# Edge messages of a graph layer: pairs of edges on a partition, gathers without a wait for TensorE, a deeper order of weighing and summing

## The chip, the cores and the metric

The kernel runs on one core of a Trainium2 chip. The time is the device time of one execution in microseconds. Shown are 4624.53, 4624.89 and 4639.22 us, with a median of 4624.89 us, and one execution taken by the profiler, 4628.1 us.

Engines are called as in the profile: PE (TensorE, matmuls; PEld its weight loads), DVE (VectorE), ACT (ScalarE), POOL (GpSimd) and SP (SyncE). SBUF is the working memory, PSUM the memory into which TensorE writes. A semaphore is a counter by which one engine tells another that something is done.

## The reference

12500 nodes with 128 features, and 412500 edges: 200000 random ones in both directions, and one edge from each node to itself. The edges are sorted by their target `dst`, so a target has 33 edges in a row on average.

```python
theta = x[dst] - x[src]
w = sigmoid(relu(theta @ W1 + b1) @ W2 + b2)          # one number for each edge
agg = segment_sum(w * theta, dst, num_segments=n_nodes)
indeg = segment_sum(ones, dst, num_segments=n_nodes)
x = layernorm(x + agg + indeg * (x @ W4 + b4))
```

All is in 32-bit floats. An edge from a node to itself has theta = 0 and adds nothing to `agg`, and 1 to `indeg`.

## The kernel before

**Tables.** `theta @ W1` is `y[dst] - y[src]` with `y = x @ W1`, so `y` is computed once for all nodes. `z` in DRAM holds y and x of a node side by side (1 KB), `y3d` holds y split in three bf16 parts, from which a bf16 matmul makes the full value again.

**Parts and blocks.** The sorted edges are cut into parts, and two parts are a block (`SUB`). A block has a window of 96 consecutive targets (`WB`). The first 20 parts (`PLAIN`) have 1024 edges each. Each later part takes CE = 1182 consecutive edges: 1024 of them are laid out as 8 tiles (`K`) of 128 edges, an edge to a partition, and up to 128 others are "hot": edges whose source is one of the first 2304 nodes, whose rows lie in SBUF (`tabs`), so that they need no gather. Edges from a node to itself are dropped (except for the first 20 parts). There are 352 parts, 351 whole ones and a tail.

**Planning.** Which edge of a part goes where is computed on the chip, by `place` (L451), in sets of 128 parts, a part to a partition. It finds the hot edges (`max` and `match_replace` on 1182 columns, L511 and L513), counts how far each remaining edge has to move, moves them by powers of two (L572 to L576), and hands out `src_i` (the sources, for the gathers), `rel` (the target within the window) and the rows `off_d` (the target within the part), which are read back from DRAM, broadcast to all partitions, as `to_all` (L688). It is a generator, and the main loop takes a step of it now and then.

**One part,** in the main loop over s (L1069 on):

- `gather(s + 4)` (L335 to L353): eight indirect DMAs issued by POOL, each with 128 rows of z into one tile of a buffer. There are nine such buffers, `zbuf`, used in turn.
- `one_hot(s + 2)` (L772, L773): ACT makes from `to_all` a matrix that picks each edge's target, |offset - place| and then 1 - that, cut at zero, for 8 tiles and one of hot edges, 1152 columns.
- `spread_y(s + 1)` (L781): eight matmuls that bring y of the target to each edge, into `ph` (PSUM, two buffers).
- `one_hot_w(s)` (L791): DVE compares the target in the window with 0 to 95, 768 columns.
- `weights(s)`: DVE subtracts the gathered y (L824), masks and multiplies with W2 (L825), sums over the features (L828); ACT makes the sigmoid, once for the multiplication (`gate`, L829), once as a column of `wx` (L830).
- `weigh(s)` (L839): DVE multiplies the gathered x with the weight into `wx` (two buffers). It is the last to read the part's zbuf.
- `add_up(s - 1)` (L940): eight matmuls sum the weighted rows by target into `pa`, one more adds the hot edges, and in a block's second part one carries on the sums of targets that the last block shared (`sh`). A 32-bit matmul is two instructions in the profile. `total` copies `pa` to SBUF (L951).
- `hot_weights(s + 1)` (L915 to L920), `hot_rows(s + 2)` (L904, L905), and every four parts `hot_fetch` (L884, L891, L895), which picks 512 hot rows by 27 matmuls.
- once in a block `own_u` (L707 to L714) for the targets' own term, and `normalize` (L963 to L990), which finishes the block two before.

**Order.** SP's queue is in the order of the program; a scheduler of the language arranges the other engines' instructions ahead of time by its own estimate, and every engine runs its own in that fixed order. Loads of a block are issued on SP two blocks ahead (L670 to L698). POOL's queue holds nothing but gathers. They are paced by hand: each gather of part s is made to wait for an instruction of TensorE that belongs to the work of part s - 6:

```python
if s - LAG >= NH and (s - LAG, k) in steps_of:
    waits.append((steps_of[s - LAG, k], mybir.DependencyClass.Sync))
```

`step(...)` writes these instructions down in own_u, spread_y, hot_rows and add_up.

Of the kernel before, what the change touches and what calls it, by code (L numbers as in the profile page):

```python
# [19 lines left out]
P = 128  # L20
D = 128
K = 8
BE = K * P
# [7 lines left out]
NZ = 9  # L31
AHEAD = 4
LB = 6
LAG = 6
# [8 lines left out]
RW = BE + HK  # L43
# [5 lines left out]
CE = 1182  # L49
# [7 lines left out]
def gnn_resnorm(  # L57
# [45 lines left out]
    KT = -(-TAIL // P)  # L103
    assert NS == NF + 1 and NS % SUB == 0 and TAIL <= BE and SUB == 2 and N < BIG

# [36 lines left out]
    def load(i):  # L142

        s0, n, full = sets[i]
        es = ep.tile([P, CE], I32, name="es")
        ed = ep.tile([P, CE + 1], I32, name="ed")
        e0 = E1 + (s0 - PLAIN) * CE
        if full < n:
            nc.vector.memset(es[:n, :], 0)
            nc.vector.memset(ed[:n, :], N)  # L150
# [68 lines left out]
    oh_buf = [const.tile([P, K + 1, P], BF16, name=f"oh{i}") for i in range(2)]  # L219
# [78 lines left out]
    wx_buf = [const.tile([P, K, AW], F32, name=f"wx{i}") for i in range(2)]  # L298
# [3 lines left out]
    wxh_buf = [const.tile([P, AW], F32, name=f"wxh{i}") for i in range(3)]  # L302
# [15 lines left out]
    def tiles(s):  # L318
        return K if s < NF else KT
# [9 lines left out]
    steps_of = {}  # L329
    table_steps = []  # L330

    def step(s, i, ins):

        steps_of[s // SUB * SUB + i // K, i % K] = ins

    def gather(s):

        (src_i, _, _), i = set_of(s)
        for k in range(tiles(s)):
# [7 lines left out]
            if s - LAG >= NH and (s - LAG, k) in steps_of:  # L347
                waits.append((steps_of[s - LAG, k], mybir.DependencyClass.Sync))
# [92 lines left out]
    def place(i, ps, es, ed, bb):  # L441
# [9 lines left out]
        c = ep.tile([P, 6], F32, name="col")[:n]  # L451
# [9 lines left out]
        v.tensor_scalar(b[:full, 1:2], c[:full, 3:4], -1.0, float(CE - BE - HR * HS),  # L461
                        op0=OP.mult, op1=OP.add)
# [5 lines left out]
        t = ep.tile([P, CE], F32, name="et")[:n]  # L468
        nc.scalar.activation(t, ed[:, :CE], AF.Identity, scale=float(BIG), bias=c[:, 0:1])
        C = CE // 3  # L470
        for j in range(3):
            at = slice(j * C, (j + 1) * C)
            step = ps.tile([P, G, P], F32, name=bank).rearrange("p g d -> p (g d)")[:n, :C]
            v.tensor_sub(step, ed[:, j * C + 1:(j + 1) * C + 1], ed[:, at])
            q = ep.tile([P, P * G], F32, name="eq")[:n, :C]
            v.tensor_sub(q, es[:, at], ed[:, at])
            v.tensor_mul(q, q, step)
            v.scalar_tensor_tensor(t[:, at], step, 0.0, t[:, at], op0=OP.is_equal, op1=OP.mult)
# [11 lines left out]
        key = ep.tile([P, CE + 1], F32, name="ed")[:n, :CE]  # L490
# [3 lines left out]
        for r in range(HR):  # L494
            apart = aparts[r][:n]
            whole = CE // PM * PM
# [3 lines left out]
                apart.rearrange("p (o m) -> p o m", o=1).to_broadcast([n, CE // PM, PM]), op=OP.add)  # L500
            if whole < CE:
                v.tensor_tensor(key[:, whole:], t[:, whole:], apart[:, :CE - whole], op=OP.add)
# [32 lines left out]
        nc.sync.dma_start(rows_d[:n, BE:], hd[:, 1, :])  # L535
        hots[s0] = hot_s, hrel, n

        w = ep.tile([P, CE], I32, name="ew")[:n]
        C = CE // 6
        for j in range(6):  # L540
            at = slice(j * C, (j + 1) * C)
            pw = ps.tile([P, G, P], F32, name=bank).rearrange("p g d -> p (g d)")[:n]
            count = pw[:, :C]
            q = ep.tile([P, P * G], F32, name="eq")[:n]
            keep, out_ = q[:, :C], q[:, C:2 * C]
# [4 lines left out]
            v.tensor_tensor_scan(count, out_, most[:n].to_broadcast([n, C]),  # L550
                                 c[:, 4:5] if j else 0.0, op0=OP.add, op1=OP.min)
            v.tensor_copy(c[:, 4:5], count[:, C - 1:])
            move = out_.bitcast(I32)
            far_on = pw[:, C:2 * C]
# [6 lines left out]
        v.tensor_sub(b[:full, 10:11], c[:full, 4:5], c[:full, 3:4])  # L561
        v.tensor_scalar(b[:full, 10:11], b[:full, 10:11], -float(HR * HS), None, op0=OP.add)
        v.tensor_scalar(b[:full, 11:12], b[:full, 10:11], -1.0, None, op0=OP.mult)
        assert SW + HR * HS < LAST + P
        for r, m in enumerate([1 << r for r in range(7)] + [LAST]):
            u = ep.tile([P, CE], I32, name="ew" if r % 2 else "et")[:n]
            C = bits.shape[1] - m
            for c0 in range(0, CE, C):
                c2 = min(c0 + C + m, CE)
# [9 lines left out]
                if c2 == CE:  # L579
                    break  # L580
            w = u
        to = ep.tile([P, CE + 1], I32, name="ed")[:n, :BE]
        v.tensor_scalar(to, w[:, :BE], BIG.bit_length() - 1, 2 * NOT - 1,
                        op0=OP.logical_shift_right, op1=OP.bitwise_and)
        off = ep.tile([P, P * G], F32, name="eq").bitcast(BF16)
        nc.scalar.activation(off[:n], to, AF.Identity, bias=c[:, 1:2])
        nc.sync.dma_start(rows_d[:n, :BE], off[:n])
        yield
        t = ep.tile([P, CE], F32, name="et")[:n]
        nc.scalar.activation(t[:, :BE], to, AF.Identity, bias=c[:, 2:3])  # L590
        src_i = pp.tile([P, K, P], I32, name="src_i")
        rel = pp.tile([P, K, P], BF16, name="rel")
        f = ep.tile([P, CE], F32, name="es")[:n]
# [3 lines left out]
        for e, to in ((f, src_i), (t, rel)):  # L597
            for k0 in range(0, K, G):
                pt = ps.tile([P, G, P], F32, name=bank)
                for j in range(G):  # L600
                    nc.tensor.transpose(pt[:, j, :n], e[:, (k0 + j) * P:(k0 + j + 1) * P],
                                        ident[:n, :n])
                nc.scalar.activation(to[:, k0:k0 + G, :n], pt[:, :, :n], AF.Copy)
# [3 lines left out]
    with tc.manual_schedule(engines={SP}), tc.tile_pool(name="work", bufs=2) as wp, tc.tile_pool(  # L607
# [94 lines left out]
        def own_u(b):  # L702
# [3 lines left out]
            step(b * SUB - 2, 2,  # L706
# [593 lines left out]
```

## Time and profile before

| | |
|---|---|
| median of 3 runs | 4624.89 us (4624.53 to 4639.22) |
| profiled execution | 4628.1 us, span 4626.2 us |
| PE busy, PEld busy | 2636.8 us (57%), 1988.8 us (43%) |
| DVE busy | 3121.2 us (67%) |
| ACT busy | 1603.8 us (35%) |
| POOL busy | 2681.1 us (58%), 2815 gathers |
| TensorE clock granted, mean | 0.729 |
| moved by DMA | 539.42 MB, 117 GB/s |

The clock of TensorE is at all times either whole or half, and 0.729 is the mean. A group's row gives line, engine, operation, tile written and tiles read, sizes, count, then busy time and the mean of one in ns, then the idle time of the engine before these instructions, with what ended most of it. "issue" is time in which the engine waited for nothing that the profile shows. "remote" stands where a semaphore rose and the profile found no instruction that ended at that moment. A line of the waits has who waited, for whom, the total in us, how many times, and the longest.

### The profile page before, as it was taken

How to read it: one execution, taken by the hardware profiler on the slowest of the kernel's cores; microseconds unless marked ns; L12 is line 12 of the kernel's file. 1: busy time of each engine (PE TensorE's matmuls, PEld its weight loads, DVE VectorE, ACT ScalarE, POOL GpSimd, SP SyncE). 2: the span in 40 equal slices, each digit the busy share in tenths (PEclk: the TensorE clock that was granted, in tenths of full speed). 3: DMA queues.
4: the chain of work that ended last, by engine and by line, in shares of the span. 5: the costliest groups of instructions: out<-in, count | busy, mean ns of one | idle time of the engine just before them, and what ended most of it. 6: DMA issues, size and time to landing. Idle time of an engine off the chain costs nothing. (4 is left out here: it accounts for less than half of the span.)

```text
span 4626.2 us, 47225 instructions
## 1 busy us (share of the span) xinstructions
PE 2636.8 (57%) x14207; PEld 1988.8 (43%) x14207; DVE 3121.2 (67%) x5030; ACT 1603.8 (35%) x3344; POOL 2681.1 (58%) x2824
## 2 busy tenths in 40 slices
PE   4355556665655555655565655556555556555555
PEld 4344344444444444444444444444444444444444
DVE  5676667777776666666777776777666566566666
ACT  4233333333333333333333333333333333333333
POOL 4415656666565566665556656656656565655663
PEclk6676777767777777777777777776777777777777
DMA  6303433443443344434333433434433443333432
GB/s 247 111 28 108 126 115 114 122 121 112 118 122 110 109 125 122 120 114 122 112 118 116 121 109 115 123 111 123 121 112 112 121 120 117 116 116 114 120 113 67
DMA packets 269164, 539.42 MB, mean 117 GB/s; under 512 B 101349, under 2 KB 152737, under 8 KB 267365
## 3 DMA queue, kind: packets, MB, share of 16 engines
q0 software_dynamic: 134096, 364.95, 27.2%
q1 hardware_dynamic: 132834, 164.97, 11.2%
q10 hardware_dynamic: 1970, 6.40, 0.5%
q8 instruction: 115, 1.88, 0.2%
q14 instruction: 149, 1.21, 0.1%
HBM read 504.19 MB, written 31.90 MB: 116 GB/s over the span
## 5 line engine op out<-in xcount | busy, mean ns | idle before, releaser
L340 POOL DMA_INDIRECT zbuf<-z,src_i x2655 | 2524.2, 951 | 1645.1 <-issue 695.5
L940 PE MATMUL pa<-wx,ow 128*96 128x130 f32 x5630 | 1125.8, 374 | 847.3 <-ACT a L951 339.9
L940 PEld LDWEIGHTS pa<-wx,ow 128*96 128x96 f32 x5630 | 1006.2, 238 | 953.9 <-ACT a L951 366.8
L839 DVE TENSOR_TENSOR wx<-zbuf,fix 128x1024 f32<-128x1024 f32 x352 | 427.3, 1214 | 601.0 <-ACT fix L829 449.2
L772 ACT ACTIVATE oh<-to_all,away 123x1152 bf16<-123x1152 bf16 x332 | 415.7, 1252 | 689.8 <-remote 350.2
L891 PE MATMUL pd<-of,tabs 128*128 128x512 bf16 (+1 forms) x2322 | 543.1, 385 | 91.2 <-issue 90.7
L791 DVE TENSOR_TENSOR ow<-fix,rel 128x768 f32<-128x768 f32 x352 | 333.5, 947 | 300.3 <-remote 296.7
L884 DVE TENSOR_TENSOR of<-hot_src,fix 128x1536 bf16<-128x1536 f16 (+1 forms) x258 | 422.2, 1690 | 10.8 <-remote 8.6
L828 DVE TENSOR_REDUCE lg<-ph 128x8 f32<-128x1024 f32 x352 | 427.0, 1213 | 0.0
L824 DVE TENSOR_TENSOR ph<-ph,zbuf 128x1024 f32<-128x1024 f32 x344 | 420.2, 1222 | 8.8 <-issue 3.2
L904 PE MATMUL pw<-wni,xT 128*128 128x256 f32 x664 | 301.7, 548 | 210.1 <-ACT wxh L918 106.2
L825 DVE SCALAR_TENSOR_TENSOR ph<-ph,w_r 128x1024 f32<-128x1024 f32 x344 | 420.7, 1223 | 0.0
L891 PEld LDWEIGHTS <-tabs 128*128 128x128 bf16 x2322 | 233.1, 101 | 363.3 <-issue 150.5
L773 ACT ACTIVATE oh<-oh 123x1152 bf16<-123x1152 bf16 x332 | 384.1, 1157 | 6.4
L781 PE MATMUL ph<-y,oh 128*128 128x128 bf16 x2751 | 261.0, 244 | 180.5 <-DVE lg L828 121.3
L781 PEld LDWEIGHTS <-oh 128*128 128x128 bf16 x2751 | 215.7, 111 | 246.5 <-issue 211.5
L915 DVE SCALAR_TENSOR_TENSOR hh<-pw,w_r 128x128 f32<-128x128 f32 x332 | 92.6, 279 | 285.5 <-PE pw L905 181.2
L940 PE MATMUL pa<-a,sh 96*96 96x130 f32 x350 | 106.2, 398 | 287.7 <-issue 85.4
L963 ACT ACTIVATE pw<-xw,sw 96x128 f32<-96x128 f32 x176 | 64.6, 367 | 545.2 <-issue 241.4
L904 PEld LDWEIGHTS pw<-wni,xT 128*128 128x128 f32 x664 | 142.7, 266 | 246.4 <-ACT wxh L918 135.9
L895 ACT ACTIVATE xT<-pd 128x512 f32<-128x512 f32 (+1 forms) x86 | 50.1, 582 | 481.6 <-PE pd L891 388.4
L951 ACT ACTIVATE a<-pa 96x130 f32<-96x130 f32 x176 | 47.8, 272 | 459.4 <-remote 398.5
(257 smaller groups left out, 2925.5 us busy)
## 6 DMA issues: line engine op xcount, KB each, us to landing
to_all<-off_d SPq DMA_DIRECT2D x166, 576.0 KB
zbuf<-z,src_i POOLq DMA_INDIRECT x2655
z<-zbuf SPq DMA_DIRECT2D x12, 1024.0 KB
y<-y3d SPq DMA_DIRECT2D x342, 30.8 KB
y3d<-tabs SPq DMA_DIRECT2D x12, 768.0 KB
xw<-in_x_dram SPq DMA_DIRECT2D x176, 48.0 KB
out_dram<-o SPq DMA_DIRECT2D x176, 48.0 KB
zbuf<-in_x_dram ACTq DMA_DIRECT2D x12, 512.0 KB
```

Source lines behind the costliest of these rows:

```text
L340: ins = nc.gpsimd.indirect_dma_start(out=rows_of(s)[:, k, :], out_offset=None, in_=z if s >= NH else x, in_offset=IndirectOffsetOnAxis(ap= ...
L772: nc.scalar.activation(gap, at[:3 * SW, h], AF.Abs, bias=away[:3 * SW])
L773: nc.scalar.activation(gap, gap, AF.Relu, scale=-1.0, bias=1.0)
L781: got = nc.tensor.matmul(d["ph"][:, k, :], d["oh"][:, k, :], blocks[b]["y3"][h], start=True, stop=True)
L824: nc.vector.tensor_sub(ph, ph, zs[:, :n, :D])
L825: nc.vector.scalar_tensor_tensor(h[:, :n, :], ph, 0.0, w2_f.to_broadcast([P, n, D]), op0=OP.max, op1=OP.mult)
L828: summed = nc.vector.tensor_reduce(lg[:, :n], h[:, :n, :], AX.X, OP.add)
L839: return nc.vector.tensor_tensor(wx_buf[s % 2][:, :n, :D], xs[:, :n, :], w.to_broadcast([P, n, D]), op=OP.mult)
L884: nc.vector.tensor_tensor(of, hot_src[:, r, lo:hi].rearrange("p (o e) -> p o e", o=1).to_broadcast([P, T, hi - lo]), nid[:, g * T:(g + 1) ...
L891: nc.tensor.matmul(px, tabs[:, r, g * T + t, c, :], of[:, t, :], start=g == 0 and t == 0 and c == 0, stop=g == 2 and t == T - 1 and c == 2)
L904: nc.tensor.matmul(px[:, :2, :], xT, wni, start=True, stop=False)
L940: summed = nc.tensor.matmul(pa, one, w, start=h == 0 and i == 0, stop=h == 1 and i == len(terms) - 1)
```

## The change

Seven things change together.

1. **Pairs.** In parts behind the first 20, an edge and the next one with the same target share a partition: tile k and tile k + 4 (`J` = 4) hold the two sources, and there is one offset and one place in the window for the pair. A target left with an odd number of edges keeps its edge to itself, which adds nothing to the sum, as the last one's partner. `spread_y` makes four matmuls for a part, and the subtraction reads their result twice; `one_hot` has 640 columns, `one_hot_w` 384; `add_up` has four matmuls with 260 columns, the two halves side by side, into a `pa` of 2 x 130, and the two halves are added in `finish`. The `to_all` rows are shorter. How many edges a partition stands for comes from `rel`'s second half and is copied to `wx`'s last column.
2. **Planning.** `place` finds the pairs: a scan that alternates within a target's row, and a mark for each edge that needs a neighbour. It works in eight pieces for six, with seven more operations in each.
3. **Size.** CE is 1156 for 1182, and each part gets one column more; there are 360 parts for 352.
4. **No pace.** `LAG`, `steps_of` and `step` are gone; a gather waits for the list of its sources and for its buffer.
5. **Weighing** of part s - 1 comes behind the weights of part s.
6. **Summing** of part s - 2 comes in iteration s; `finish` and `normalize` follow later.
7. **Buffers.** `wx` has three, `wxh` and `owh` four, `ow` four of half the size.

```diff
-LAG = 6
+NW = 3
-CE = 1182
+CE = 1156
+WE = CE + 1
...
-            if s - LAG >= NH and (s - LAG, k) in steps_of:
-                waits.append((steps_of[s - LAG, k], mybir.DependencyClass.Sync))
...
@@ place
+            v.scalar_tensor_tensor(mark, t[:, at], float(BIG), keep, op0=OP.is_ge, op1=OP.add)
+            v.tensor_scalar(mark, mark, -1.0, 1.0, op0=OP.mult, op1=OP.add)
+            if j:
+                v.tensor_copy(odd[:, :1], c[:, 5:6])
+            else:
+                v.memset(odd[:, :1], 0.0)
+            v.tensor_tensor_scan(odd[:, 1:], mark, keep, c[:, 5:6] if j else 0.0,
+                                 op0=OP.mult, op1=OP.add)
+            v.tensor_copy(c[:, 5:6], odd[:, m:])
+            v.scalar_tensor_tensor(mark, mark, 0.0, odd[:, :m], op0=OP.is_equal, op1=OP.mult,
+                                   accum_out=c[:, 6 + j:7 + j])
+            v.tensor_add(keep, keep, mark)
...
@@ one_hot
-                gap = oh[:3 * SW]
+                gap = oh[:3 * SW, :J + 1]
...
@@ spread_y
-            for k in range(tiles(s) if s >= NH else 0):
-                got = nc.tensor.matmul(d["ph"][:, k, :], d["oh"][:, k, :], blocks[b]["y3"][h],
-                                       start=True, stop=True)
+            n, k0 = (K, 0) if s < PLAIN else (pairs(s), J)
+            for k in range(n if s >= NH else 0):
+                nc.tensor.matmul(d["ph"][:, k0 + k, :], d["oh"][:, k, :], blocks[b]["y3"][h],
+                                 start=True, stop=True)
...
@@ weights
+                if s >= PLAIN:
+                    n = pairs(s)
+                    y = y[:, J:J + n, :].rearrange("p (o k) d -> p o k d", o=1)
+                    y = y.to_broadcast([P, 2, n, D])
...
+                nc.vector.tensor_sub(to, y, zy)
...
+            if s >= PLAIN:
+                (_, rel, _), i = set_of(s)
+                nc.scalar.activation(wx[:, J:, D + 1:], rel[:, J:, i:i + 1], AF.Copy)
...
@@ add_up
-                bd["pa"] = ps_l.tile([P, AW], F32, name="pa")
+                bd["pa"] = ps_l.tile([P, 2, AW], F32, name="pa")
...
-            terms = [(d["ow"][:, k, :], wx_buf[s % 2][:, k, :]) for k in range(n)]
+            wx = wx_buf[s % NW]
+            if s < PLAIN:
+                terms = [(d["ow"][k // J][:, k % J, :], wx[:, k, :]) for k in range(K)]
+            else:
+                wx = wx.rearrange("p (h k) d -> p k h d", h=2)
+                terms = [(d["ow"][0][:, k, :], wx[:, k]) for k in range(pairs(s))]
...
+        def finish(b):
+
+            d = blocks[b]
+            a = d["a"]
+            if b * SUB >= PLAIN:
+                nc.vector.tensor_add(a[:WB], a[:WB], d["pa"][:WB, 0, :])
...
@@ the main loop
-                summed = weights(s)
-                weighted = [summed]
+                weighted = [weights(s)]
+                if PLAIN < s:
+                    weighted.append(weigh(s - 1))
...
+            if s % SUB and 0 < b <= PLAIN // SUB:
+                finish(b - 1)
             if s % SUB == 0 and b > 1:
-                with after(weighted if s == NS else []):
+                if b - 2 < PLAIN // SUB:
                     normalize(b - 2)
+                else:
+                    finish(b - 2)
+            if s % SUB and b - 2 >= PLAIN // SUB:
+                normalize(b - 2)
...
-            if s < NS - 1:
+            if s < PLAIN:
                 weigh(s)
-            if s > 0:
-                with after(weighted if s >= NS else []):
-                    add_up(s - 1)
+            if 0 <= s - 1 < PLAIN:
+                add_up(s - 1)
+            if PLAIN <= s - 2 and s < NS:
+                add_up(s - 2)
```

More of the change, by code (lines that the diff above doesn't have):

```diff
@@ L316, in gnn_resnorm, with pairs, slots, filled @@
     NX = NH // 2
[L318 to L319 removed]
+    def pairs(s):
+        return J if s < NF else JT
+    def slots(s):
+        return [h * J + j for h in range(2) for j in range(pairs(s))]
+    def filled(t, s):
+        if s < NF:
+            return t
+        return t.rearrange("p (h j) d -> p h j d", h=2)[:, :, :JT, :]
     def rows_of(s):
@@ L939, in add_up @@
             for i, (one, w) in enumerate(terms):
-                summed = nc.tensor.matmul(pa, one, w, start=h == 0 and i == 0,
-                                          stop=h == 1 and i == len(terms) - 1)
-            step(s + 1, (13, 5)[h], summed)
+                to = pa if len(w.shape) == 3 else pa[:, 0, :]
+                nc.tensor.matmul(to, one, w, start=h == 0 and i == 0,
+                                 stop=h == 1 and i == len(terms) - 1)
             if h:
@@ L1098, in gnn_resnorm @@
         with after(weighted):
+            normalize(NK - 2)
+            add_up(NS - 2)
+            add_up(NS - 1)
+            finish(NK - 1)
             normalize(NK - 1)
```

199 lines of the change are left out of this document (105 added, 94 removed).

## The prediction

> **What bounds the kernel now.** I read the page's busy times and costliest groups first, then busy time in one long window, then the waits of POOL, then the timeline around the longest waits.
>
> ```profile
> PE 2636.8 (57%) x14207; PEld 1988.8 (43%) x14207; DVE 3121.2 (67%) x5030; ACT 1603.8 (35%) x3344; POOL 2681.1 (58%) x2824
> ...
> L340 POOL DMA_INDIRECT zbuf<-z,src_i x2655 | 2524.2, 951 | 1645.1 <-issue 695.5
> L839 DVE TENSOR_TENSOR wx<-zbuf,fix 128x1024 f32<-128x1024 f32 x352 | 427.3, 1214 | 601.0 <-ACT fix L829 449.2
> L772 ACT ACTIVATE oh<-to_all,away 123x1152 bf16<-123x1152 bf16 x332 | 415.7, 1252 | 689.8 <-remote 350.2
> L791 DVE TENSOR_TENSOR ow<-fix,rel 128x768 f32<-128x768 f32 x352 | 333.5, 947 | 300.3 <-remote 296.7
> L828 DVE TENSOR_REDUCE lg<-ph 128x8 f32<-128x1024 f32 x352 | 427.0, 1213 | 0.0
> L824 DVE TENSOR_TENSOR ph<-ph,zbuf 128x1024 f32<-128x1024 f32 x344 | 420.2, 1222 | 8.8 <-issue 3.2
> L825 DVE SCALAR_TENSOR_TENSOR ph<-ph,w_r 128x1024 f32<-128x1024 f32 x344 | 420.7, 1223 | 0.0
> ```
>
> No engine is full. But a gather that POOL issues (L340) takes 0.95 us and is followed by 0.30 us of issue, 1.25 us in all, and a part needs eight: 10.0 us that POOL can't shorten. The window of 500 to 4500 us:
>
> ```profile
> 500.00:4500.00 4000.00, 2322.82 (x12428) 1730.30 (x12426) 2704.94 (x4289) 1383.78 (x2913) 2422.58 (x2549) 0.74 0.40 117
> ```
>
> The columns are PE, PEld, DVE, ACT and POOL, busy us with the count. 2549 gathers are 318.6 parts, so a part takes 12.55 us: 10.0 us of gathers and 2.55 us (812 us in the window) in which POOL stands still. DVE's own need is 2704.94/318.6 = 8.5 us a part. POOL's gathers and pauses set the pace. What ends the pauses:
>
> ```profile
> POOL zbuf L340 <- issue: 734.6, 2345, 4.4
> POOL zbuf L340 <- PE pd L707: 422.6, 72, 16.1
> POOL zbuf L340 <- remote: 312.1, 140, 3.9
> POOL zbuf L340 <- PE ph L781: 164.0, 23, 83.9
> POOL zbuf L340 <- PE pa L940: 77.8, 30, 22.1
> POOL zbuf L340 <- PE pw L905: 62.4, 67, 6.4
> ```
>
> All but the first line is TensorE (every wait shown as "remote" here is on TensorE's semaphore): these are the waits that the change removes, 1039 us of them. Why they are not simply a gift is in the timeline:
>
> ```profile
> 1668.01 0.94 POOL L340 DMA_INDIRECT zbuf<-z,src_i  x1 [6.36 <-PE pw L905]
> 1676.07 0.61 PE L781 MATMUL ph<-y,oh 128*128 128x128 bf16 x8
> 1678.31 0.46 PE L940 MATMUL pa<-a,sh 96*96 96x130 f32 x2 [1.64 <-issue]
> ...
> 1690.52 0.94 POOL L340 DMA_INDIRECT zbuf<-z,src_i  x1 [0.30 <-issue]
> 1694.85 0.96 DVE L791 TENSOR_TENSOR ow<-fix,rel 128x768 f32<-128x768 f32 x1 [16.09 <-remote]
> 1694.99 0.28 ACT L951 ACTIVATE a<-pa 96x130 f32<-96x130 f32 x1 [16.14 <-remote]
> 1695.23 0.95 POOL L340 DMA_INDIRECT zbuf<-z,src_i  x1 [3.77 <-remote]
> ```
>
> POOL issues 19 gathers without a break, 1668.0 to 1691.5. TensorE finishes the block's sum at 1678.8. ACT, which only waits for that sum, starts at 1695.0, with DVE and POOL: TensorE's signal came 16 us after its work, and 3.4 us after POOL had stopped. It is the rule of this trace. After 500 us I counted the moments when TensorE's semaphore rose: while POOL had issued without a break for less than 6 us, 540 of 605 came within 0.1 us of the end of a matmul that signals; between 6 and 9 us, 62 of 130; between 9 and 18 us, 10 of 142. The first signal after a run of gathers comes 2.1 us behind its end for runs of 12 to 15 us, 2.6 at 17 to 19, 3.4 at 21 to 25. DVE's and ACT's signals are not held up. So POOL's pauses are also when everybody else hears of TensorE.
>
> **The change, part by part.**
>
> *More gathers.* CE falls from 1182 to 1156, so 392020 edges behind the first 20 parts fill 339 whole parts and a tail of 136: 360 parts for 352. Gathers: 359x8 + 2 = 2874 against 2655 + 96 + 64 = 2815. 59 x 1.25 = +74 us of issue, on the path, since nothing covers POOL. With them come eight parts of DVE work (8 x 8.5 = 68 us) and four blocks of loads on SP's queue, beside POOL.
>
> *Pairs.* TensorE's L781 drops from eight matmuls to four (0.61 us for eight), L940 from 16 instructions of 130 columns (1.99 us in the timeline at full clock) to 8 of 260; the nearest row, L904 with 256 columns, has 548 ns where 130 columns have 374, pipeline included, so the sum of that group lies between 0.7 and 1.0 of the old. ACT's two passes over the one-hots shrink from 1152 to 640 columns: between the rows of 1152 (1.25 and 1.16 us) and 512 (0.68 and 0.63), 0.80 and 0.73, so -0.88 us, and a new copy of 128x4 costs at most the 0.29 of L830. DVE's L791 halves to 384: 0.55 us by the slope between 768 (0.95) and 1024 (1.21), -0.40; the new add of two halves per block is a 96x130 add, 0.29 by the 96x128 row of L964, +0.14 a part. L824 now reads half of its input broadcast: 1.22 stays, as for L825, which broadcasts already; not below, since the output is as large. None of this is on POOL's path: 0 us, covered by POOL's 10.0 us a part. Were POOL gone, DVE's 8.5 - 0.26 = 8.2 us would be the bound.
>
> *Planning (place).* Per set, six passes of ten small operations become eight of seventeen; at 0.27 to 0.36 us each and 0.63 for a scan, narrower now, that is about +19 us of DVE. Two of the three sets run under POOL's pace: 0. The first runs in the opening, where DVE was busy two thirds of the time (66 to 77% between 100 and 400 us): +12 us, between 0 and 19.
>
> *End.* Two sums, a finish and a normalize stand behind the last weights: +3 us, between 0 and 8 by the 1.99 us row of L940.
>
> *Waits of gathers removed; weighing one part later, sums two later, wx three deep.* Now a gather waits only until DVE has weighed the part nine before (zbuf has nine buffers). DVE's signal is prompt, so POOL no longer stops for TensorE: the 812 us go. What is late next: POOL is faster than DVE (10.0 us against what DVE gets done), so it fills all nine buffers and then waits for DVE; and DVE waits for TensorE's signals, held up for as long as POOL runs. A cycle then is: POOL stops on a full ring; 3.4 us later (the longest row above; longer runs may add to it) TensorE's signals arrive; DVE does sub, mask, reduce and the weighing behind them, 1.22 + 1.22 + 1.21 + 1.21 = 4.9 us; a buffer is free and POOL goes on. A stop costs 8.3 us, where before POOL went on the moment TensorE was heard. So what counts is how many parts N lie between stops.
>
> N: from the release, DVE frees a buffer at 4.9 us and, at 8.2 us a part, at 13.1, 21.3 and 29.5; POOL, running from 4.9, needs them by 14.9, 24.9 and 34.9, so it doesn't pause. TensorE goes unheard from about 4.9 + 9 = 14 us. The L781 of a part is issued when the reduce two parts before is done (ph has two buffers), so what was heard by 14 us carries DVE through two more subs; the third buffer is sure, the fourth hangs on ACT, whose queue has L951 and the copies of own_u, both waiting for TensorE, ahead of the next gate. N = 3 or 4; I take 3.5, a pause of 8.3/3.5 = 2.37 us a part. 318.6 + 59/8 = 326 parts x 2.37 = 773 us, -39 against 812. Bounds: N = 3, 2.77 us, 903 us, +91; N = 4, 2.08 us, 678 us, -134.
>
> SP's queue is held up in these stretches too (a DMA on it that issues in 0.34 us elsewhere, and the steps between, took 0.70 each from 1684 to 1690); its blocks are fetched two ahead, so 0, and with longer runs it may become the late one.
>
> **Sum** on the profiled execution, span 4626.2 us and 1.9 around it (4628.1, 0.07% over the median of 4624.89): +74 - 39 + 12 + 3 = +50, so 4678 us.
>
> **Rivals.**
>
> *Faster: the deeper pipeline carries DVE through the unheard stretch.* The sums and weights of a part may now be one and two parts late, and L839's 449 us behind ACT's gate are gone. If DVE goes six parts between stops, the pause is 8.3/6 = 1.38 us a part, 450 us, -362: 4355 us. It decides from N = 3.75, where the pauses saved (2.22 us a part) pay the added gathers. For it: at 1678 DVE stood at L791 only because its two buffers were still read, and there are four now. Against: ph still has two buffers, and L781 needs the reduce. In the extreme POOL never pauses: 4628 - 812 + 89 = 3905 us. The Trainium skill (SBUF — State Buffer, Who interferes with whom) says that a DMA never contends with a compute engine and that TensorE shares no SBUF port; by that the gathers could hold nobody up and this extreme would be near. The trace, with 16 us between TensorE's end and its signal, bears it out little.
>
> *Much slower: N near 2.5.* If ACT's queue stops at L714 or L951 each block, DVE gets only the third buffer every other time: 8.3/2.5 = 3.32 us a part, 1082 us, +270: 4987 us. At N = 2, with 2.95 + 4.9 a stop, 5185. For it: ACT stands longest behind TensorE (398.5 us at L951). Against: gates no longer have to be in time for the same part's weighing.
>
> *No change in the pauses.* The waits change their name only, 2.55 us a part: 326 x 2.55 = 831, +19 + 89, 4736 us; it lies inside my own range.
>
> **How the numbers follow.** N = 3 to 4, 4583 to 4808 us: 0.47. N above 4, around 4355: 0.36. N below 3: 0.17. A kernel of this kind repeats to about 0.3%, so no change means 4611 to 4639 us. Of my own case 0.07 lies under that and 0.06 in it. Faster 0.36 + 0.07 = 0.43, same 0.06, slower 0.34 + 0.17 = 0.51. Signs are thus nearly even; the single likeliest value is 4678. To leave out no more than 0.2, the range goes to 4330 (most of the faster case) and 4960 (half of the slow one).
>
> **What the profile after would show.** POOL's waits name DVE's L839 line, no TensorE; runs of gathers of 30 to 40 us with stops of about 8 us; L340 2874 gathers at 0.95; DVE's L791 near 0.55; ACT's pair near 1.5 us. Runs of 60 us or none of the late TensorE signals make me wrong towards fast; runs of 20 us with 8 us stops towards slow; so does SP, if DVE or ACT is found waiting for to_all.

## The result, and the profile after

The changed kernel takes 5095.57 us (median of 4, 5087.38 to 5099.05) against 4624.71 us for the kernel before in the same runs: a ratio of 1.1012, 95% interval 1.0981 to 1.1042. It is slower by a tenth. (These runs, like those of the trace before, are of a kind in which TensorE's signals are late; some of the last experiments met another.) The profiled execution took 5087.38 us, span 5085.5, which is 459 us more than the profiled execution before.

The page of the changed kernel, busy times and the groups that answer to those shown of before:

```profile
PE 2521.3 (50%) x10431; PEld 1545.7 (30%) x10431; DVE 3114.5 (61%) x5543; ACT 1431.7 (28%) x3755; POOL 2744.4 (54%) x2883
...
L349 POOL DMA_INDIRECT zbuf<-z,src_i x2714 | 2586.3, 953 | 2028.6 <-issue 768.1
...
L876 DVE TENSOR_TENSOR wx<-zbuf,fix 128x1024 f32<-128x1024 f32 x360 | 437.7, 1216 | 899.0 <-ACT fix L863 751.0
...
L797 ACT ACTIVATE oh<-to_all,away 123x640 bf16<-123x640 bf16 x340 | 279.6, 822 | 606.5 <-remote 340.9
...
L798 ACT ACTIVATE oh<-oh 123x640 bf16<-123x640 bf16 x340 | 249.7, 734 | 8.5
L868 ACT ACTIVATE wx<-rel 128x4 f32<-128x4 bf16 x340 | 70.5, 207 | 586.7 <-remote 250.8
L817 DVE TENSOR_TENSOR ow<-fix,rel 128x384 f32<-128x384 f32 x380 | 205.9, 544 | 27.3 <-remote 25.8
```

TensorE, DVE and ACT do less than before, POOL 63 us more (its added gathers), and all stand still longer. POOL's idle time before gathers rose from 1645 to 2029 us, and the weighing (L876, L839 before) waits 751 us for its gate where it waited 449. The same window as before, with the columns PE, PEld, DVE, ACT, POOL:

```profile
500.00:4500.00 4000.00, 2002.48 (x7985) 1186.25 (x7983) 2450.43 (x4292) 1104.58 (x2986) 2233.57 (x2342) 0.71 0.34 98
```

2342 gathers are 292.75 parts, so a part takes 13.66 us where it took 12.55. A gather still takes 1.25 us with its issue. So the loss is in POOL's pauses, and the waits of POOL and ACT say who ends them:

```profile
POOL zbuf L349 <- issue: 918.8, 2646, 36.6
...
POOL zbuf L349 <- DVE wx L876: 736.1, 92, 25.9
...
ACT pw L1012 <- issue: 558.2, 48, 21.4
...
POOL zbuf L349 <- DVE st L1022: 426.3, 63, 13.7
...
ACT oh L797 <- remote: 340.9, 41, 23.6
ACT pw L1012 <- remote: 297.9, 29, 20.8
...
ACT wx L868 <- remote: 250.8, 50, 22.2
...
ACT a L993 <- remote: 42.2, 6, 12.8
```

TensorE is all but gone from POOL's waits, as intended (58 us are left), and DVE stands there: the weighing, or BatchNorm statistics issued just behind a weighing. "Remote" has moved to ACT. From 500 us to 80 us before the end I measured POOL's runs (gathers with under 0.7 us between them) and the stops that end them:

| | before | after |
|---|---|---|
| runs, mean length | 242, 13.1 us | 166, 19.8 us |
| mean stop | 3.65 us | 7.34 us |
| stop per part | 2.74 us | 3.68 us |
| parts between stops (N) | 1.3 | 2.0 |
| TensorE's signals within 0.1 us, run younger than 6 us | 538 of 603 | 362 of 365 |
| 6 to 9 us | 62 of 130 | 51 of 63 |
| 9 to 18 us | 10 of 142 | 14 of 75 |
| 18 us and more | 0 of 2 | 3 of 137 |

The runs of the changed kernel are of two kinds: 80 of 9 to 12 us (one part) and 73 of 25 to 35 us (three parts). They alternate, and the timeline shows what happens in each:

```profile
2063.76 1.22 DVE L876 TENSOR_TENSOR wx<-zbuf,fix 128x1024 f32<-128x1024 f32 x1 [5.80 <-ACT fix L863]
2065.25 0.95 POOL L349 DMA_INDIRECT zbuf<-z,src_i  x1 [7.34 <-DVE st L1022]
2065.77 5.07 DVE L921 TENSOR_TENSOR of<-hot_src,fix 128x1536 bf16<-128x1536 f16 x3
...
2067.89 8.09 PE L928 MATMUL pd<-of,tabs 128*128 128x512 bf16 x27
...
2076.56 0.60 ACT L932 ACTIVATE xT<-pd 128x512 f32<-128x512 f32 x1 [3.69 <-PE pd L928]
...
2078.99 1.22 DVE L876 TENSOR_TENSOR wx<-zbuf,fix 128x1024 f32<-128x1024 f32 x1 [2.74 <-ACT fix L863]
...
2080.49 0.95 POOL L349 DMA_INDIRECT zbuf<-z,src_i  x1 [5.52 <-DVE wx L876]
...
2084.33 1.22 DVE L876 TENSOR_TENSOR wx<-zbuf,fix 128x1024 f32<-128x1024 f32 x1 [0.36 <-ACT yu L739]
...
2092.06 1.21 DVE L876 TENSOR_TENSOR wx<-zbuf,fix 128x1024 f32<-128x1024 f32 x1
...
2093.19 0.22 PE L942 MATMUL pw<-y,oh 128*128 128x128 bf16 x1
...
2109.29 0.95 POOL L349 DMA_INDIRECT zbuf<-z,src_i  x1 [0.30 <-issue]
2113.56 0.37 ACT L1012 ACTIVATE pw<-xw,sw 96x128 f32<-96x128 f32 x1 [20.77 <-issue]
...
2115.81 1.21 DVE L876 TENSOR_TENSOR wx<-zbuf,fix 128x1024 f32<-128x1024 f32 x1
...
2117.29 0.95 POOL L349 DMA_INDIRECT zbuf<-z,src_i  x1 [7.05 <-DVE st L1022]
```

Four parts take 2117.29 - 2065.25 = 52.0 us and hold two stops. The weighings, each of which frees one buffer, come at 2063.76, 2078.99, 2084.33, 2092.06 and 2115.81, so 15.2, 5.3, 7.7 and 23.8 us apart. The first gap is the fetch of the rows from the table in SBUF (`hot_fetch`), which comes once in four parts: 5.07 us on DVE, 8.09 us on TensorE, and a copy in ACT's queue (L932) ahead of the next gate. POOL has gathered one part by then and stands for 5.5 us. The last gap is the unheard TensorE: POOL gathers three parts without a break from 2080.49 to 2110.2; TensorE is done at 2093.4 with the tile that L1012 writes into (L941 and L942 make the rest of it); ACT goes on at 2113.56, 20 us after that and 3.3 us after POOL stopped. The row of L1012 says "issue" because ACT's sequencer, not ACT, stood there: from 2092.50 on it waited for TensorE's semaphore and for that of a load that landed at 2096.4, and TensorE's rose at 2113.49.

This is the pattern of the whole trace, not of one stretch: the fetch begins on DVE during 73 of the 80 short runs, and during 1 of the 73 long ones. The stops behind short runs take 7.3 us on average (median 5.6), those behind long runs 6.7 (6.1).

### The profile page after: what moved, and what is told of

The parts are those of the page before. It is cut to its first block, busy times and chain, and to the rows that moved or that the text cites. A ratio compares the mean times of both kernels' runs of the same rounds, so it can differ in the third digit from the quotient of the medians.

```text
span 5085.5 us, 39606 instructions
## 1 busy us (share of the span) xinstructions
PE 2521.3 (50%) x10431; PEld 1545.7 (30%) x10431; DVE 3114.5 (61%) x5543; ACT 1431.7 (28%) x3755; POOL 2744.4 (54%) x2883
## 4 chain that ended last, share of the span: by engine, by line
PE 28%; issue 21%; another core or an unknown queue 20%; DVE 16%; ACT 12%; DMA 1%; SPq 1%; POOL 0%; DVEq 0%; ACTq 0%; POOLq 0%
PE pd L928 12%; PE pa L980 9%; DVE wx L876 5%; PE pw L941 3%; ACT oh L797 2%; ACT oh L798 2%; DVE lg L862 2%; DVE ph L857 1%; PE pd L736 1%; DVE ph L856 1%; ACT wxh L953 1%; ACT xT L932 1%; PE pd L732 1%; ACT wxh L952 1%
## 5 line engine op out<-in xcount | busy, mean ns | idle before, releaser
L349 POOL DMA_INDIRECT zbuf<-z,src_i x2714 | 2586.3, 953 | 2028.6 <-issue 768.1
L980 PE MATMUL pa<-wx,ow 128*96 128x260 f32 (+1 forms) x3034 | 986.2, 479 | 264.2 <-DVE wx L876 114.6
L876 DVE TENSOR_TENSOR wx<-zbuf,fix 128x1024 f32<-128x1024 f32 x360 | 437.7, 1216 | 899.0 <-ACT fix L863 751.0
L980 PEld LDWEIGHTS pa<-wx,ow 128*96 128x96 f32 x3034 | 594.8, 214 | 517.3 <-issue 181.3
L928 PE MATMUL pd<-of,tabs 128*128 128x512 bf16 (+1 forms) x2376 | 655.2, 444 | 31.4 <-issue 27.2
L807 PE MATMUL ph<-y,oh 128*128 128x128 bf16 x1453 | 166.7, 248 | 776.6 <-DVE lg L862 427.6
L941 PE MATMUL pw<-wni,xT 128*128 128x256 f32 x680 | 309.7, 548 | 316.6 <-ACT wxh L953 168.6
L797 ACT ACTIVATE oh<-to_all,away 123x640 bf16<-123x640 bf16 x340 | 279.6, 822 | 606.5 <-remote 340.9
L807 PEld LDWEIGHTS <-oh 128*128 128x128 bf16 x1453 | 121.8, 112 | 827.1 <-issue 799.6
L1012 ACT ACTIVATE pw<-xw,sw 96x128 f32<-96x128 f32 x180 | 66.0, 366 | 915.5 <-issue 558.2
L941 PEld LDWEIGHTS pw<-wni,xT 128*128 128x128 f32 x680 | 142.1, 260 | 368.1 <-ACT wxh L953 207.8
L798 ACT ACTIVATE oh<-oh 123x640 bf16<-123x640 bf16 x340 | 249.7, 734 | 8.5
L868 ACT ACTIVATE wx<-rel 128x4 f32<-128x4 bf16 x340 | 70.5, 207 | 586.7 <-remote 250.8
L817 DVE TENSOR_TENSOR ow<-fix,rel 128x384 f32<-128x384 f32 x380 | 205.9, 544 | 27.3 <-remote 25.8
```

The lines of the kernel that those rows point to most:

```text
L349: ins = nc.gpsimd.indirect_dma_start(out=rows_of(s)[:, k, :], out_offset=None, in_=z if s >= NH else x, in_offset=IndirectOffsetOnAxis(ap= ...
L797: nc.scalar.activation(gap, at[:3 * SW, h], AF.Abs, bias=away[:3 * SW])
L798: nc.scalar.activation(gap, gap, AF.Relu, scale=-1.0, bias=1.0)
L807: nc.tensor.matmul(d["ph"][:, k0 + k, :], d["oh"][:, k, :], blocks[b]["y3"][h], start=True, stop=True)
L876: return nc.vector.tensor_tensor(filled(wx_buf[s % NW][:, :, :D], s), xs, w.to_broadcast(list(xs.shape)), op=OP.mult)
L928: nc.tensor.matmul(px, tabs[:, r, g * T + t, c, :], of[:, t, :], start=g == 0 and t == 0 and c == 0, stop=g == 2 and t == T - 1 and c == 2)
```

## The experiments

All ratios are to the kernel before in the same set of runs, with 95% intervals. In three sets the kernel before took 4629, 4764 and 4641 us; in two others it took 3721 and 3724 us; these two stand near the end, and the set with 4641 is the last.

**Only the pace taken away.**

```diff
--- before
-            if s - LAG >= NH and (s - LAG, k) in steps_of:
-                waits.append((steps_of[s - LAG, k], mybir.DependencyClass.Sync))
```

> The kernel before with one part of the change alone: gathers no longer wait for TensorE's steps. Theory (the lost pace costs: without it POOL gathers on until its ring of buffers is full, TensorE's signals are not seen meanwhile): slower than before by 5 to 11%, 4860 to 5130 us; runs of gathers grow from 13.1 us to 18 us and more on average, the stops name DVE's L839 in place of TensorE, and the pause per part rises from 2.74 us to 3.4 to 3.9. Rival (pairs or the late weighing cost, the pace does nothing for the time): 4610 to 4640 us, as before.

Measured: 5304.44 us, 1.1470 (1.1442 to 1.1498), worse than the theory said. Its waits, POOL's and the longest others:

```profile
POOL zbuf L340 <- DVE owh L918: 1198.1, 132, 15.8
POOL zbuf L340 <- issue: 837.1, 2566, 18.9
ACT a L949 <- remote: 745.2, 65, 22.8
ACT xT L893 <- remote: 533.6, 43, 16.0
```

Runs grew to 18.0 us, stops to 8.69 us, 4.71 us per part. The instructions of TensorE, DVE and ACT come in the same order as in the kernel before (14207, 5030 and 3344 of them), so the program was not arranged anew; it only waits elsewhere. One part of the change, two lines, does more harm than the whole. The other parts together are worth a gain once the pace is gone: 1.1012 against 1.147, 4%.

**The changed kernel with the pace put back.**

```diff
--- after
+            if s - LAG >= NH and (s - LAG, k) in steps_of:
+                waits.append((steps_of[s - LAG, k], mybir.DependencyClass.Sync))
...
@@ add_up, and likewise in own_u, spread_y, hot_rows
+                step(s + 2, (5, 13)[h], got)
```

> The changed kernel with the pace put back (a gather again waits for the TensorE steps of the part six before it, the summing's step at its new place two parts later). Theory (the lost pace costs): most of the loss comes back, 4590 to 4780 us, runs of gathers near 13 us again, pause per part near 2.7. Rival (late weighing and the ACT copy in front of the gate cost): 5040 to 5110 us, since they are still there.

Measured: 4720.21 us, 1.0197 (1.0170 to 1.0224). Of the 10.1% four fifths are back. Stops are 3.82 us, 2.70 per part, as before the change. Three of its waits:

```profile
DVE wx L887 <- ACT fix L874: 708.0, 150, 29.4
POOL zbuf L355 <- PE pd L741: 486.5, 88, 21.7
ACT wx L879 <- remote: 428.2, 55, 19.5
```

POOL stops for TensorE again (the second line). The wait for the gate is nearly as long as in the changed kernel (708 us for 751), that of ACT's copy longer (428 for 251), and the time is back all the same: these waits were not what it went to.

**The weighing and summing at their old places, too.** With the pace back, what is left is the pairs, the 59 more gathers and the further buffers. `finish` and `normalize` go back to their old places with the two shown here.

```diff
--- after, with the pace
-                if PLAIN < s:
-                    weighted.append(weigh(s - 1))
...
-            if s < PLAIN:
+            if s < NS - 1:
                 weigh(s)
-            if 0 <= s - 1 < PLAIN:
+            if s > 0 and s < NS:
                 add_up(s - 1)
-            if PLAIN <= s - 2 and s < NS:
-                add_up(s - 2)
```

> The changed kernel with the pace put back as in the paced one (4720 us) and, besides, the weighing and the summing back at their old places (rows weighted in their own part, summed one later): of the change only the pairs, the 59 more gathers and the third buffer are left. If the 91 us that the paced kernel is over the kernel before are the pairs' (59 gathers at 1.25 us are 74 us, 12 us are more placing): 4690 to 4740 us. If they are the later weighing's (the weighing waits 708 us for the gate in the paced kernel, 449 in the kernel before): 4600 to 4660 us.

Measured: 1.0162 (1.0137 to 1.0187), 4842 us where the kernel before takes 4764. In ratio that is as good as the paced kernel, whose interval it overlaps. The remaining 2% is left with the pairs and their larger number of parts: 59 more gathers at 1.25 us are 74 us, of 78 us between 4842 and 4764. The later weighing is worth nothing that these runs can tell while the pace is there.

**ACT's copy out of the gate's way.**

```diff
--- after
@@ weights
-                nc.scalar.activation(wx[:, J:, D + 1:], rel[:, J:, i:i + 1], AF.Copy)
...
@@ the main loop, ahead of add_up(s - 2)
+                ends(s - 1)
```

> The changed kernel with ACT's copy of the second ends (L868, which waits for the summing three parts before) moved out of the way of the gate: it is issued one part later, ahead of the summing that needs it. Theory (the lost pace costs, the copy is one of several places where an unheard TensorE shows): 5000 to 5110 us, the wait of the weighing for the gate shrinks and another wait for TensorE grows in its place. Rival (this copy at the head of ACT's queue is the new stall): 751 us of waits for the gate fall under 450, and the time to 4750 to 4900 us.

Measured: 1.0996 (1.0959 to 1.1034), no change. N is 2.0 again and the weighing waits 790 us for the gate. The copy was one of several places in ACT's queue where an unheard TensorE shows; the stall is not its own. The wait for the gate didn't shrink, which the expectation had wrong.

**Rests.** POOL fills a scratch tile after each four gathers, and waits for nothing.

```diff
--- after
+            for _ in range(5 if s >= NH and k % 4 == 3 else 0):
+                ins = nc.gpsimd.memset(rest, 0.0)
...
+                gathers.append(ins)
```

> The changed kernel with a rest in POOL's queue after each four gathers: POOL fills a scratch tile of 128x128 five times (0.204 us each in the trace of before, 1.0 us or a little more together), twice a part, and waits for nothing. Theory (TensorE goes unheard only when gathers run without a break for over 6 to 9 us): runs are cut at 5 us, TensorE's signals are seen at once, waits put down to remote nearly vanish, and a part takes POOL's 10.0 us + 2 rests = 12.0 to 12.6 us: 4450 to 4680 us, 8 to 12% faster than the changed kernel though POOL is given more to do. Rival (POOL stops because DVE and ACT are late for a reason of their own): the rests are eaten by the 3.7 us per part in which POOL idles anyway: 5050 to 5110 us.

Measured: 4704.93 us, 0.9882 (0.9863 to 0.9902). It is faster than the kernel before, which took 4764 in this set. The changed kernel was not in this set; at 1.1012 it would be at 5246 (4764 x 1.1012), so the rests gain 10%, by giving POOL 734 us more to do. (The bounds of the expectation were meant for a kernel before at 4625.) Its groups and its longest wait:

```profile
L350 POOL DMA_INDIRECT zbuf<-z,src_i x2714 | 2588.8, 954 | 856.4 <-issue 823.7 <-DVE of L929 23.8 <-DVE ow L825 1.0
...
L363 POOL MEMSET rest<- 128x128 f32 x3510 | 733.7, 209 | 161.8
```

```profile
DVE ph L864 <- DMA zbuf<-z,src_i: 1296.4, 247, 10.5
```

POOL hardly waits for anybody, 1215 of 1218 of TensorE's signals come within 0.1 us, and DVE waits for rows: POOL is the bound, at 12.7 us a part. DVE and ACT run the same instructions in the same order as in the changed kernel (5543 and 3755), and breaks in POOL's queue alone bring the signals back and the time down. So it is shown that in this kind of runs long runs of gathers make TensorE's signals late, and that the changed kernel's loss comes from it; by what way they do it is not shown.

**One rest of double size a part.**

```diff
--- after, with rests
-            for _ in range(5 if s >= NH and k % 4 == 3 else 0):
+            for _ in range(10 if s >= NH and k % 8 == 7 else 0):
```

> The same rest in sum, but in one piece: ten fills after each eight gathers, so that a run is at least 10 us. If it is the unbroken run that counts and not POOL's load, this does clearly worse than two rests of half the size: TensorE goes unheard for the last 3 us or so of each run and is heard again 1.6 us after its end (9 to 12 us runs of the changed kernel), 4650 to 4950 us. If only the sum of POOL's idle time counts: as with two rests, within 1%.

Measured: 1.0019 (1.0008 to 1.0031), 1.5% slower than two rests (4773.69 against 4704.93). Of TensorE's signals 181 of 257 are prompt at a run's age of 6 to 9 us, and 42 of 81 behind that. The age of the run counts, but a 10 us run does less harm than I had thought, as long as a sure break of 3 us follows each.

**Half the bytes.**

```diff
--- after
+    for t in zbuf[NX + 3:]:
+        nc.vector.memset(t, 0.0)
...
-                out=rows_of(s)[:, k, :], out_offset=None, in_=z if s >= NH else x,
+                out=rows_of(s)[:, k, :D], out_offset=None, in_=x,
```

> The changed kernel with gathers of the same number and the same 128 rows, but of 512 bytes each in place of 1024 (they read the 128 columns of x, and the second half of each row in the buffer stays as it was, so the values are not the reference's). If POOL's issuing of descriptors is what keeps TensorE unheard: the table of signals by age of the run stays (prompt under 6 us, hardly any over 12 us), and the time stays at 4950 to 5120 us. If the bytes do it (the queues that fetch the rows are full): signals stay prompt for twice as long, and the time falls under 4800 us.

Measured: 1.1278 (1.1254 to 1.1302). The DMA lines of the two pages, this kernel's first, then the changed kernel's:

```profile
DMA packets 230002, 320.89 MB, mean 60 GB/s; under 512 B 103600, under 2 KB 156482, under 8 KB 228232
```

```profile
DMA packets 274961, 505.04 MB, mean 99 GB/s; under 512 B 103600, under 2 KB 156482, under 8 KB 273192
```

With 36% fewer bytes TensorE is heard no better: 59 of 152 at 6 to 9 us, 20 of 152 at 9 to 18, none of 57 beyond. So it isn't the bytes of the rows. What stayed the same is POOL's issuing and the number of rows asked for; no run here has one without the other, so they are not told apart. That this kernel is 2.4% slower than the changed one (1.1278 against 1.1012, from two sets) was not expected by either side and stays open.

**Smaller rests.** Two fills after four gathers, one after four, one after two, and two after four in the kernel before without its pace.

```diff
--- after, with rests
-            for _ in range(5 if s >= NH and k % 4 == 3 else 0):
+            for _ in range(2 if s >= NH and k % 4 == 3 else 0):
...
+            for _ in range(1 if s >= NH and k % 4 == 3 else 0):
...
+            for _ in range(1 if s >= NH and k % 2 == 1 else 0):
```

> The changed kernel with a smaller rest: two fills after each four gathers in place of five. With five, a part took 12.6 us of POOL's time from end to end (2501.89 to 2514.51 us) and VectorE waited 1296 us for rows, so POOL sets the pace there; six fills a part less at 0.254 us are 1.5 us, 11.1 us per part. Theory (a short break is enough, the age of the run decides): TensorE is still heard at once and the time falls by up to 360 x 1.5 = 547 us, to 0.87 to 0.93 of the kernel before. If the break must outlast some drain (the first signal comes 1.06 us after a run of 5 us): signals go unheard again and the time is 1.00 to 1.10 of the kernel before.

> The changed kernel with one fill of 0.25 us after each four gathers, 10.6 us of POOL's time per part. If any break at all is enough: 0.85 to 0.92 of the kernel before. If the break must be of about the 1.06 us that a first signal takes after 5 us of gathers: heard no better than without rests, 1.03 to 1.10. I expect the second here, since gathers have pauses of 0.30 us between them already.

> The changed kernel with one fill of 0.25 us after each two gathers: as much rest per part as two fills after four, in twice as many pieces. If rest in sum counts, as with two fills after four, within 1%; if the single break must be long enough, worse than these by 3% and more.

> The kernel before without its pace (1.147 of the kernel before by itself), with two fills after each four gathers in place of it. Theory (the pace worked only by making breaks in which TensorE is heard, so rests do as well or better): 0.90 to 0.98 of the kernel before, and 2 to 6% slower than the changed kernel with the same rests, since rows are weighted in their own part and VectorE has eight one-hot columns to make in place of four. Rival (the old kernel needs the wait on TensorE's steps for its order of work): above 1.05.

This set met something else: the kernel before took 3721 us there, and 1.1185, 1.0366, 1.0520 and 1.0906 are ratios to that. In these traces TensorE's signals are prompt at any age of a run (1858 of 1858 behind more than 40 us of gathers with one fill after four). So the set gave no verdict on the rests, but showed that the effect is not always there. The two kernels themselves, in another set of the same kind:

> The kernel before once more, for its trace beside the changed kernel's on the same chip. Where it takes about 3721 us: signals of TensorE prompt also behind 9 to 18 us of gathers (10 of 142 in the first trace), pauses of gathers well under 1 us per part where they were 2.74. Where it takes 4600 to 4800 us: as in the first trace.

> The changed kernel once more. In the run with small rests the kernel before took 3721 us in place of 4625 to 4764, and TensorE's signals were prompt at any age of a run (1858 of 1858 behind more than 40 us of gathers), so the unheard TensorE is not there on every chip. If this run meets such a chip: POOL's gathers set the pace at 10.0 us per part and the 59 more of them cost 74 us, 3690 to 3850 us, 0.99 to 1.035 of the kernel before, in place of 1.10. If it meets one like the first (kernel before at 4600 to 4800 us): 1.095 to 1.105 again.

Measured: before 3724.18 us (its profiled execution 3721.28), after 3799.86 us, 1.0201 (1.0184 to 1.0218). The windows of before and of after:

```profile
500.00:3500.00 3000.00, 2066.57 (x11610) 1556.15 (x11683) 2538.63 (x4029) 1305.10 (x2721) 2271.67 (x2392) 0.80 0.49 146
```

```profile
500.00:3500.00 3000.00, 1995.04 (x8069) 1196.93 (x8141) 2482.75 (x4356) 1130.24 (x3042) 2272.58 (x2389) 0.78 0.46 133
```

2392 and 2389 gathers in 3000 us are 10.03 and 10.05 us per part: POOL issues from end to end without one pause of 0.7 us, in the kernel before with its pace too. There the change is slower for one reason: 59 more gathers at 1.254 us are 74 us, of 81 us between the spans. What pairs save on TensorE, ACT and DVE is beside POOL and worth nothing. The rests there only add to POOL's time, twice the same:

> Two fills after each four gathers, against the kernel before. On a chip where the kernel before takes 4600 to 4800 us: if the age of the run decides, 0.87 to 0.95; if the break must be over the 1.06 us of the first signal, 1.00 to 1.10. On a chip where it takes about 3721 us: 1.11 to 1.13 again, since the rests only add to POOL's time there.

> One fill after each four gathers. On a chip where the kernel before takes 4600 to 4800 us: if any break is enough 0.85 to 0.92, else 1.03 to 1.10, and I expect the second. On a chip where it takes about 3721 us: 1.03 to 1.045 again.

Measured: 1.1172 and 1.0355.

**Smaller rests where TensorE goes unheard.** The last set had the kernel before at 4641 us.

> Two fills after each four gathers, once more, for a chip on which TensorE goes unheard (kernel before at 4600 to 4800 us): if the age of the run decides, 0.87 to 0.95 of the kernel before; if the break must be over the 1.06 us that the first signal takes there behind four gathers, 1.00 to 1.10. Where the kernel before takes about 3720 us: 1.117 again.

> The kernel before with two fills after each four gathers in place of its pace. Where TensorE goes unheard: if such rests are enough, 0.87 to 0.98 and near the changed kernel with the same rests; if not, 1.05 to 1.15, as without any pace (1.147). Where the kernel before takes about 3720 us: 1.09 again.

> The kernel before without its pace. Where TensorE is heard at any age of a run (kernel before at about 3720 us, POOL without a pause): the pace has nothing to do there, and taking it away changes nothing, 0.997 to 1.003. Where TensorE goes unheard: 1.14 to 1.15 again.

Measured: 1.0556 (1.0532 to 1.0581), 1.0942 (1.0909 to 1.0976) and 1.1431 (1.1399 to 1.1463). With two fills, gathers of 4.7 us are parted by breaks of 0.63 to 0.99 us, and only 451 of 930 signals are prompt in the changed kernel, though no stretch of gathers between two breaks is older than 6 us. A run's age as such is thus not the whole rule: breaks of 0.63 to 0.99 us do not end a run, those of five fills (1.4 to 1.8 us) do. Where between 1.0 and 1.4 us it turns was not measured. The 1.06 us of the expectations is no such limit: it is the median of the first signal in those breaks of five fills in which one came (156 of 655), and 148 of these came within 0.1 us of the end of their matmul. It tells when the next matmul ended, not how long a signal was held up. Two fills take away nearly half of the changed kernel's loss (5.6% for 10.1%) and a third of that of the kernel before without its pace (9.4% for 14.3%), and a sure break has to be paid for: five fills give 1.2% over the kernel before in the one set where they ran (kernel before at 4764 us), and where TensorE is heard two already cost 9.5% (1.1172 against 1.0201). No kernel tried here is the best in both.

## Why the prediction was wrong, by its steps

**More gathers, +74: right.** It is 59 x 1.254 in either kind of run, and where TensorE is heard it is nearly the whole difference.

**Planning +12: near; end +3: too small.** The 241st gather is issued 13.2 us later than before (539.6 against 526.4 us); I put that down to the planning ahead of it. What follows the last gather takes 69.2 us for 56.7, +12.5 where I had 3, bounded at 8.

**Pairs, 0: right,** as far as the kernels with the pace put back tell. The sizes came out: L817 0.544 us (0.55), ACT's pair 0.82 + 0.73 (0.80 + 0.73).

**Unheard TensorE: right.** The first signal comes 3.8 us after runs of 25 to 35 us (3.4 taken from 21 to 25 us). A stop costs 7.3 us on average, and 6.7 behind the runs of 25 to 35 us, where I had 8.3.

**Parts between stops, N = 3.5: this step failed.** It is 2.0. I let DVE free a buffer each 8.2 us, the mean of a part. But DVE's work is uneven: the fetch from the table comes every fourth part, and with its copy in ACT's queue it sets the next weighing 15.2 us behind the last. POOL, with one buffer free, uses it up in 10 us and stops, though TensorE is heard. The three parts that I called sure did come in the next run, and no fourth. So four parts hold two stops, in the stretch shown of 5.5 and 7 us. What held ACT was little the block's sum and the copies of `own_u`, as I had put it (L993 has 42 us of remote waits, L734 and L739 31 us together), but the one-hots (L797, 341 us), the own-term of `normalize` (L1012, 298 us, and 558 under "issue", of which the stretch shown has one) and the copy to `wx` (L868, 251 us). That the fetch is what ends the short runs is read from the trace; no run moved or removed it. The pauses came to +332 us from the 241st gather on (880.8 to 1212.8), where I had -39.

With N and the stop as measured the prediction's formula comes near: 7.34 / 2.0 = 3.67 us a part, x 326 = 1196 us, +384 against 812, and 4628 + 384 + 89 = 5101 us, for 5087 measured. The nearness is in part luck: a stop of 7.34 us has in it the 0.30 us that stand before any gather, which the 812 us have not. Of the 459 us the 332 of pauses, 74 of gathers, 13 ahead of the 241st gather and 12 of the end are named. The other 28 come of that same 0.30 us: there are 78 fewer stops, so 78 more of the plain spaces of 0.305 us between two gathers (24 us), and a gather takes 0.953 us for 0.951 (some 5 us). The N = 2 of the second rival (5185 us) was the nearest, but for another reason than its own: it had ACT stop at L714 or L951. The sign named for a kernel that is too slow, runs of 20 us with stops of 8 us, is what came on the mean (19.8 and 7.3 us). I had given N under 3 a chance of 0.17, because a gate no longer had to be in time for its own part. The long runs, of three parts, bear that reason out; the fetch was not in it.

**The extreme without pauses, 3905 us,** was called little borne out by the trace. It is what happens where TensorE is heard, 3800 us; but the kernel before loses its pauses there as well, which no trace of before could show. The Trainium skill (SBUF — State Buffer, Who interferes with whom) states that a DMA never contends with a compute engine. The runs in which TensorE is heard agree with it: behind 500 us all 1790 of TensorE's signals are prompt in the second trace of the kernel before, while POOL gathers without a pause. The others neither bear it out nor speak against it: TensorE's signals are late there, with half the bytes too, but no run here shows a contention on SBUF.

SP, which I had named as a possible late one, was not: ACT waited 18.5 us in all for `to_all`, though its steps take 0.71 us in the long runs of the changed kernel here too (2102 to 2104 us).

## What to carry to other kernels

A wait in the profile can be work for somebody else: ask what reaches the other engines while the waiting one is still, before you take it away. When a ring of buffers is to bridge a stall, count with the longest distance between two releases, not with their mean; with a fetch in one part of four, N was 2.0 here and not 3.5. And where an engine's issue sets the pace, count its instructions first: 59 more gathers cost 74 us, nearly 2%, whatever else was saved.

## What was not expected of the hardware

The same two programs have two speeds, by the set of runs: 4616 to 4779 us and 3720 to 3729 us for the kernel before, 5095.57 and 3799.86 us for the changed one. In the one kind TensorE's signals are late behind gathers, in the other never. POOL's gathers take 0.95 + 0.30 us in both. In the late kind what counts is how long a break is: 1.4 to 1.8 us behind each four gathers are enough, 0.63 to 0.99 us are not. What makes a set be of the one kind or the other isn't in the traces, and stays open. It is not the chip alone, as an expectation above took it to be: the same chip (number 11) had a set at 4764 us and a later one at 3721 us. The granted clock of the kernel before differs too (0.72 to 0.74 in the late kind, 0.78 to 0.79 in the other); whether that is a cause or a result, no run here tells. The way by which runs of gathers hold TensorE's signals back stays open as well. A measured gain of such a kernel is to be read together with which kind it met: taking the pace away costs 14 to 15% in the one; in the other it was not tried alone, and the pace was seen to cost no pause there.
